# Moving statistics and a normalisation from VectorE to ScalarE in a four-layer convolution kernel, with a free choice of engine behind its long layer

## Chip, cores and metric

The kernel runs on one core of a Trainium2 chip. The metric is device time in microseconds (us), the median of several runs. The engines are named as the profile names them: PE (TensorE's matmuls; PEld is its weight loads), DVE (VectorE), ACT (ScalarE), POOL (GpSimd) and SP (SyncE, which here issues the DMAs).

## What is computed

The input is x of shape (8, 32, 256, 256): eight images of 32 channels. Four layers follow, each added to its own input, and each reads a group-normalised copy of it (mean and variance over two channels and the whole image):

```python
x = x + L0(gn(x), ...)   # 1x1 convolution, then a 5x5 filter per channel, pooled from the features
x = x + L1(gn(x), w)     # 8-bit quantised: out[f] = -sum over c, kh, kw of |patch - w|
x = x + L2(gn(x), w, b)  # 3x3 convolution
x = x + L3(gn(x), ...)   # layer norm over channels in 8x8 windows, then four networks k1..k4

def fastkan(x, ln_g, ln_b, ws, wb, bb):
    ln = layernorm(x, ln_g, ln_b)
    basis = exp(-((ln[..., None] - grid) / denom) ** 2)      # 8 grid points
    return flat(basis) @ ws.T + silu(x) @ wb.T + bb
```

In L3, k1 and k2 work on two rearranged views of the normalised window y, k3 on y itself. The sum of the three is z, k4 works on z, and the layer's output is k4(z) plus the window.

L1 quantises its input: scale, clip to -127..127 and round.

## The kernel before

An image is held as 128 partitions: four blocks of 64 rows by 32 channels. Work goes by chunks of 128 x 2048 (F = 2048 words a partition). Between stages an image lies in DRAM scratch (x1, x2, x3, and q for the quantised values). Four stages are built for each image:

- **Stage 0** (`stage0`, L729). First a statistics pass over the image in 8 chunks: `add_stats` (L637, four BN_STATS of 512 on DVE, recorded at L643) and `pool` (L746, five row reductions on DVE). Small matrices follow. Then 8 chunks of convolution: 25 taps on PE into the PSUM tile psB (L892), a border correction, an eviction on ACT (L925), `add_stats` on DVE, a store to x1. At the end the image is read back in 8 pieces, scaled on ACT (L967), clipped and rounded on DVE (L972, L973) and stored to q.
- **Stage 1**, layer 1 (`stage1`, L1027). There are 16 passes (4 row blocks h by 4 groups g of 8 output channels). A pass makes 72 distance tiles max(x - w, 0) of 128 x 4128 in bf16, on DVE (L996) or in two halves on ACT (L998). Each tile is summed over channels by 8 matmuls into psA (L1018). The residual is loaded into the buffer xr and added by matmul (L1007), psA is evicted into xr on ACT (L1065), two BN_STATS read xr, and it is stored to x2.
- **Stage 2**, layer 2 (`stage2`, L1090). 8 chunks are loaded with a margin row above and below (128 x 2560) and normalised on DVE (L1131); nine taps go into psB (L1148), ACT evicts (L1164), `add_stats` reads the result, and it is stored to x3.
- **Stage 3**, layer 3 (`stage3`, L1189). There are 8 units of one chunk. For each of five layer norms `variance` (L1225) centres by matmul (recorded at L612), evicts on ACT (L1234), squares on ACT (L1239) and sums by matmul into psV (L1247); `roots` (L1256) makes the inverse root by Ln and Exp on ACT; `scale` (L1268) spreads it by matmul (L1279) and multiplies on DVE (L1287). `kan` (L1349) then makes eight basis tiles: a square on ACT (L1384, or its substitute on DVE, L1390) and an exponential on ACT (L1397); eight main matmul groups (L612) and one for the silu part add up in psB, which ACT evicts (L1462). k3 adds two tiles `oa` and `od`, the outputs of k1 and k2, which are loaded back from DRAM once the fifth exponential is done (`after=exps[4:5]`, L1430).

**What orders the work.** Nothing is ordered by hand. `Plan.add` (L126) records a task with its engine, an assumed cost in us, the buffers it reads and writes, and a rank; `Plan.run` (L229) is a list scheduler that runs once while the kernel is built and fixes each engine's order. At each moment a free engine takes the ready task of lowest rank whose buffers fit. The ranks interleave stage 1 of image b with stages 2 and 3 of image b-1 and with stage 0 of later images. The distance tiles and their matmuls of stage 1 have no rank: `Plan.fill` (L357) gives them to DVE whenever no ranked task is ready there, to PE first of all once two finished tiles wait (`URGENT = 2`) and otherwise when nothing ranked is ready, and to ACT for image 0 or after ACT has had nothing ranked for 8 us. A task with a field `other` may go to a second engine, but only once all passes of stage 1, of all images, are done (L267).

**Buffers.** `ROOM` (L68) has three tiles "bas" for basis tiles, three "si", two "rs", one "xr", and an arena "sb" of 10 F words that is allocated in pieces; `NDV = 3` tiles "dv" hold distances. A basis tile that finds no "bas" tile goes into the arena if `BASE_SPARE` words remain besides (L171). psA, psB are one PSUM tile each, psV two. The first main matmul of a basis set waits until `exps[HOLD]` is done, with `HOLD = 4`, or until no basis tile is left (L1377). For the last image `parts` (L1219) centres and spreads through psA, in halves; for the others through psB.

The normaliser's statistics end in `Norm.finish` (L647): BN_AGGR on DVE (L656), then small matmuls and DVE operations give mean and inverse deviation.

Of the kernel before, what the change touches and what calls it, by code (L numbers as in the profile page):

```python
# [24 lines left out]
R = 8  # L25
# [42 lines left out]
ROOM = [("bas", 3 * BASE, BASE), ("si", 3 * F, F), ("rs", F // 2, F // 4), ("xr", F // 2, F // 2), ("sb", 10 * F, 0)]  # L68
AHEAD = 9.0
# [5 lines left out]
BASE_SPARE = 3 * F  # L75
HOLD = 4
# [14 lines left out]
class Buf:  # L91


    def __init__(self, kind, words=0):
        self.kind, self.words = kind, words
        self.writers, self.readers = [], []
        self.tile = None
        self.left, self.first, self.at, self.taken, self.base = 0, None, None, False, kind == "bas"
        self.spill = False
# [6 lines left out]
class Plan:  # L106
# [57 lines left out]
    def fits(self, need, spare):  # L164
# [3 lines left out]
        for b in need:  # L168
            if b.kind in ("dv", "bas") and b.spill:
                b.kind = "dv" if self.places["dv"] else "bas"  # L170
            if b.base:  # L171
                b.kind = "bas" if self.places["bas"] else "sb"
                spare = BASE_SPARE
            if b.kind in self.places and not self.places[b.kind]:
                return False
# [16 lines left out]
    def bases_full(self):  # L192
        return not self.places["bas"] and sum(n for _, n in self.free["sb"]) < F + BASE_SPARE

# [34 lines left out]
    def run(self):  # L229
# [23 lines left out]
        while left or any(not p.done for p in self.passes):  # L253
            moved = True
            while moved:
                moved = False
                for e in engines:
# [3 lines left out]
                    if best is None:  # L261
                        for t in ready[e]:
# [4 lines left out]
                            if t.eng != e and not all(p.done for p in self.passes[self.first_pass :]):  # L267
                                continue
# [4 lines left out]
                        if best is not None and e == "PE" and best.rank > self.image() + AHEAD:  # L273
                            piece = self.fill(e, False)
                            if piece is not None:
                                best = piece
                        if best is not None and best.n is not None:
                            ready[best.eng].remove(best)
                            if best.other:
                                ready[best.other[0]].remove(best)  # L280
                                if best.eng != e:
                                    self.sets[best.stretch][1] -= 1
# [71 lines left out]
    def image(self):  # L354
        return next((p.b for p in self.passes[self.first_pass :] if not p.done), len(self.passes))
# [92 lines left out]
def kernel(  # L448
# [142 lines left out]
    def sb(b, n=None):  # L591
        return b.tile[:, : n or b.words] if b.tile is not None else arena[:, b.at : b.at + (n or b.words)]
# [25 lines left out]
    class Norm:  # L618
# [17 lines left out]

        def add_stats(self, src, at, r, rank, n=4):  # L637
# [8 lines left out]

        def finish(self):  # L647
# [5 lines left out]
            def first():  # L653
                for i in range(n):
# [3 lines left out]
            plan.add("DVE", 1.1 if n == 1 else 1.5, first, r=self.bufs, w=[small], rank=self.rank)  # L658
# [70 lines left out]
    def stage0(b, rank, span, after):  # L729
# [9 lines left out]
        for k in range(NCH):  # L739
            xt = Buf("sb", F)  # L740
            plan.add(
                "SP", 2.0, lambda k=k, xt=xt: by_block(lambda p, q: nc.sync.dma_start(sb(xt)[p], xn[k, q])),
# [3 lines left out]
            def pool(k=k, xt=xt):  # L746
                v = sb(xt).rearrange("p (r w) -> p r w", w=W)
# [3 lines left out]
            norm.add_stats(xt, 4 * k, [], r(0.02 * k))  # L751
            plan.add("DVE", 2.9, pool, r=[xt], w=[rs_buf[k]], rank=r(0.02 * k))
# [103 lines left out]
        for k in range(NCH):  # L856
# [60 lines left out]
            for n, t in enumerate(tap_order):  # L917
# [7 lines left out]
                lambda xt=xt: nc.scalar.activation(  # L925
                    sb(xt, F), psB.rearrange("p s f -> p (s f)"), AF.Identity, bias=bi
# [3 lines left out]
            norm1.add_stats(xt, 4 * k, [], rk)  # L930
# [23 lines left out]
        for h in range(NH):  # L954
            for j in range(0, NJ, 2):
# [15 lines left out]
                def clip(t=t):  # L971
                    nc.vector.tensor_scalar(sb(t, F), sb(t, F), QMAX, -QMAX, ALU.min, ALU.max)  # L972
                    nc.vector.tensor_scalar(q16(t), sb(t, F), ROUND, ROUND, ALU.add, ALU.subtract)  # L973

                plan.add("DVE", 2.5, clip, w=[t], rank=rk)
# [51 lines left out]
    def stage1(b, x1buf, qbuf):  # L1027
# [3 lines left out]
        for h in range(NH):  # L1031
# [16 lines left out]
            for g in range(NG):  # L1048
# [3 lines left out]
                ps.xr = xr = Buf("xr", F // 2)  # L1052
# [4 lines left out]
                            sb(xr)[p],  # L1057
# [7 lines left out]
                    lambda g=g, xr=xr: nc.scalar.activation(  # L1065
                        sb(xr), psA.rearrange("p i f -> p (i f)"), AF.Identity, bias=wsum[:, g : g + 1]
# [6 lines left out]
                norm.add_stats(xr, 8 * g + 2 * h, [], rk, 2)  # L1073
# [5 lines left out]
                            sb(xr)[p],  # L1079
# [10 lines left out]
    def stage2(b, norm, x2buf, rank, span, after):  # L1090
        im = img[b]
        r = lambda f: rank + span * f
        wc, b2 = wt[:, K0 * K0 + 2, :], cc[:, 4:5]

        def fold():
# [3 lines left out]
            nc.vector.tensor_tensor(b2, norm.mean, col(B2), ALU.add)  # L1099

# [4 lines left out]
        for k in range(NCH):  # L1105
            xt, p = Buf("sb", 10 * W), Buf("psB")
# [3 lines left out]
            def load(k=k, xt=xt):  # L1110
                d = sb(xt)
# [18 lines left out]
            def normal(xt=xt):  # L1130
                nc.vector.tensor_scalar(sb(xt), sb(xt), norm.mean, norm.rs, ALU.subtract, ALU.mult)  # L1131

            plan.add("DVE", 1.7, normal, r=[norm.done], w=[xt], rank=rk)
# [23 lines left out]
            for n, t in enumerate(taps):  # L1157
# [6 lines left out]
                lambda xo=xo: nc.scalar.activation(sb(xo, F), psB.rearrange("p s f -> p (s f)"), AF.Identity, bias=b2),  # L1164
                r=[p, sm["c2"]], w=[xo], rank=rk,
            ))
            norm3.add_stats(xo, 4 * k, [], rk)
# [21 lines left out]
    def stage3(b, norm, x3buf, rank, span):  # L1189
# [26 lines left out]
        stat = {(k, t): (Buf("psV"), Buf("rs")) for t in range(-2, U + 2) for k in "ABC"}  # L1216
        turn = lambda t: r((t + 2) / (U + 4))
        st = [dict() for _ in range(U)]
        def parts():  # L1219

            if b < nb - 1:
# [3 lines left out]
        def variance(n, t, cen, bias, rk, src, sq=None):  # L1225
# [3 lines left out]
            for p, ps, i, us in parts():  # L1229
                at = slice(i * FS, (i + (2 if us < 1 else 4)) * FS)  # L1230
                plan.add("PE", 0.85 + 0.2 * us, lambda ps=ps, i=i: cen(ps(), i), r=src, w=[p], acc=[c], rank=rk, spare=SPARE)
                plan.add(
# [6 lines left out]
            plan.add("ACT", 1.9, lambda: nc.scalar.activation(sb(sq), sb(c), AF.Square), r=[c], w=[sq], rank=rk)  # L1239
            v = stat[t][0]  # L1240
# [52 lines left out]
        def front(t, after, rk):  # L1293
# [6 lines left out]
            st[t]["c4"] = variance(4, ("A", t - 1), cen, cb, rk, [xt, sm["cenf"], sm["c3"]], xt)  # L1300

        def middle(t):

            rk = turn(t - 1.0)
# [377 lines left out]
```

## Time and profile before

| | us |
|---|---|
| median of 3 runs | 15807.77 (15794.59 to 15817.06) |
| the profiled execution | 15810.7 |
| its span, first to last instruction | 15808.7 |
| PE, DVE, ACT busy | 12814.9, 13427.1, 12262.5 |
| BN_STATS on DVE (L643) | 637.3 |
| layer 2's normalisation on DVE (L1131) | 102.8 |
| the quantiser's clip and rounding on DVE (L972, L973) | 78.2, 78.5 |

In a row of groups the columns are: line, engine, operation, tiles out<-in, shapes, count | busy time, mean length of one in ns | idle time of the engine before them, and what ended it. Busy time can be less than count times mean, since neighbours overlap.

### The profile page before, as it was taken

The numbers are of one execution on the slowest core, as the hardware profiler recorded it, in microseconds if no ns is written. First come the engines' busy times: TensorE is split into PE (matmuls) and PEld (weight loads), VectorE is DVE, ScalarE is ACT, GpSimd is POOL, SyncE is SP. The second block draws the span as 40 slices with busy tenths as digits, with TensorE's granted clock in tenths as the row PEclk, the third lists the DMA queues.
The fourth block names the chain that finished last, engine by engine and source line by source line (L and its number), as shares of the span: only waits on it lengthen the run. The fifth ranks groups of instructions, "written<-read, shape, count | busy, mean of one in ns | idle before, by whom it ended". The sixth has DMA issues, their size and how long they took to land.

```text
span 15808.7 us, 560681 instructions
## 1 busy us (share of the span) xinstructions
PE 12814.9 (81%) x260296; PEld 4330.4 (27%) x260296; DVE 13427.1 (85%) x12536; ACT 12262.5 (78%) x6849; POOL 33.1 (0%) x25
## 2 busy tenths in 40 slices
PE   6889897887897888888887888778878887887666
PEld 4223232322222222223222222222222222222222
DVE  2898989789878889888899999999999989997465
ACT  0888848678648778676778997799879987997687
POOL 0000000000000000000000000000000000000000
PEclk9989898998998999999999999999999999998777
DMA  4342345446435444554545554454544454444554
GB/s 117 74 101 55 99 118 160 108 123 169 98 97 157 130 118 125 140 139 105 133 123 142 140 131 126 114 140 123 130 127 130 127 128 129 130 132 112 148 154 134
DMA packets 1192870, 1970.85 MB, mean 125 GB/s; under 512 B 362752, under 2 KB 878848, under 8 KB 1092224
## 3 DMA queue, kind: packets, MB, share of 16 engines
q1 hardware_dynamic: 1190528, 1934.98, 46.6%
q8 instruction: 2036, 33.36, 0.9%
q14 instruction: 306, 2.51, 0.1%
HBM read 1162.83 MB, written 771.75 MB: 122 GB/s over the span
## 4 chain that ended last, share of the span: by engine, by line
PE 22%; ACT 20%; DVE 6%; issue 6%; DMA 1%; SPq 0%; DVEq 0%; ACTq 0%
PE psB L612 9%; PE psA L1018 7%; ACT bas L1384 5%; ACT bas L1397 4%; DVE dv L996 3%; ACT arena L1384 2%; PE psB L1148 2%; ACT arena L1397 2%; ACT arena L1234 2%; PE psB L892 1%; ACT si L1462 1%; ACT arena L1239 1%; DVE arena L1287 1%; PE psV L1247 1%; DVE arena L1390 1%
## 5 line engine op out<-in xcount | busy, mean ns | idle before, releaser
L996 DVE TENSOR_SCALAR dv<-qh,w1q 128x4128 bf16<-128x4128 bf16 (+1 forms) x8815 | 10491.2, 1248 | 1358.8 <-PE psA L1018 1289.9
L1018 PE MATMUL psA<-dv,sel_b 128*32 128x512 bf16 x71048 | 5420.4, 403 | 1421.8 <-DVE dv L996 1155.5
L1018 PEld LDWEIGHTS <-sel_b 128*32 128x32 bf16 x82944 | 2047.6, 97 | 6763.7 <-issue 5758.6
L1384 ACT ACTIVATE bas<-arena,kb 128x2048 f32<-128x2048 f32 x1396 | 2782.5, 1993 | 411.8 <-DVE arena L1287 258.6
L1397 ACT ACTIVATE bas<-bas 128x2048 f32<-128x2048 f32 x1396 | 2671.6, 1914 | 40.1
L998 ACT ACTIVATE dv<-qh,w1n 128x2064 bf16<-128x2064 bf16 x832 | 1635.9, 2009 | 1157.6 <-PE psA L1018 1042.0
L612 PE MATMUL psB<-bas,tl 32*32 32x512 f32 x48544 | 1953.2, 653 | 438.8 <-ACT bas L1397 240.1
L892 PE MATMUL psB<-arena,wt 32*32 32x512 f32 (+1 forms) x51040 | 1848.8, 606 | 122.2 <-issue 69.4
L612 PE MATMUL psB<-arena,tl 32*32 32x512 f32 x22368 | 918.8, 619 | 104.0 <-ACT arena L1397 29.0
L612 PEld LDWEIGHTS psB<-bas,tl 32*32 32x32 f32 x48544 | 526.5, 107 | 1327.5 <-ACT bas L1397 514.2
L892 PEld LDWEIGHTS psB<-arena,wt 32*32 32x32 f32 x51040 | 657.5, 104 | 814.0 <-issue 611.4
L1384 ACT ACTIVATE arena<-arena,kb 128x2048 f32<-128x2048 f32 x407 | 810.0, 1990 | 0.0
L1397 ACT ACTIVATE arena<-arena 128x2048 f32<-128x2048 f32 x407 | 779.1, 1914 | 11.6
L643 DVE BATCH_NORM_STATS2 tiny<-arena 128x6 f32<-128x512 f32 x768 | 473.7, 680 | 345.4 <-ACT arena L925 246.4
L1018 PE MATMUL psA<-qh,sel_b 128*32 128x512 bf16 x9216 | 666.3, 394 | 92.1 <-DMA qh<-q 76.8
L1287 DVE TENSOR_TENSOR arena<-psB,arena 128x2048 f32<-128x2048 f32 x280 | 640.0, 2286 | 59.0 <-PE psB L1279 55.9
L1462 ACT ACTIVATE si<-psB,cols_sb 128x2048 f32<-128x2048 f32 x192 | 377.0, 1963 | 385.0 <-PE psB L612 331.5
L612 PE MATMUL psB<-si,tl 32*32 32x512 f32 x14080 | 618.8, 624 | 32.4 <-DVE arena L1287 13.8
L1148 PE MATMUL psB<-arena,tl 32*32 32x510 f32 (+3 forms) x16384 | 626.6, 610 | 19.9 <-issue 19.8
L1239 ACT ACTIVATE arena<-arena 128x2048 f32<-128x2048 f32 x320 | 612.4, 1914 | 9.8
L925 ACT ACTIVATE arena<-psB,cc 128x2048 f32<-128x2048 f32 x64 | 125.6, 1962 | 536.0 <-PE psB L913 536.0
L1234 ACT ACTIVATE arena<-psB 128x2048 f32<-128x2048 f32 x224 | 418.9, 1870 | 127.1 <-PE psB L612 126.5
(151 smaller groups left out, 7406.4 us busy)
## 6 DMA issues: line engine op xcount, KB each, us to landing
arena<-x SPq DMA_DIRECT2D x128, 1024.0 KB
arena<-y SPq DMA_DIRECT2D x128, 1024.0 KB
si<-sy SPq DMA_DIRECT2D x512, 256.0 KB
arena<-in_x_dram SPq DMA_DIRECT2D x240, 384.0 KB
arena<-in_x_dram SPq DMA_DIRECT2D x256, 256.0 KB
x<-arena SPq DMA_DIRECT2D x256, 256.0 KB
xr<-x SPq DMA_DIRECT2D x512, 128.0 KB
x<-xr SPq DMA_DIRECT2D x512, 128.0 KB
```

Of the source, the lines that this page charges most:

```text
L612: nc.tensor.matmul(view(o[j * C : (j + 1) * C, i - first, :]), w_, src(rows, i, j), start=start, stop=stop)
L892: nc.tensor.matmul(o[:, lo - 2 * j : hi - 2 * j, c0:c1], wt[rows, t, :], d[rows, lo + dy + 2 : hi + dy + 2, c0 + dx : c1 + dx], start=firs ...
L996: nc.vector.tensor_scalar(dst, src, w1q[:, at : at + 1], 0.0, ALU.subtract, ALU.max)
L998: nc.scalar.activation(dst, src, AF.Relu, bias=w1n[:, at : at + 1])
L1018: nc.tensor.matmul(psA[j * C : (j + 1) * C, i, :], sel_b[:, n, :], src[:, at : at + 2, t % 3 : t % 3 + W], **flags,)
L1148: nc.tensor.matmul(o[:, lo - 2 * j : hi - 2 * j, c0:c1], (wc if t == 4 else tl[:, W2T + t, :])[rows], d[rows, lo + dy + 1 : hi + dy + 1, c ...
L1234: lambda ps=ps, at=at: nc.scalar.activation(sb(c)[:, at], ps().rearrange("p s f -> p (s f)"), func, bias=shift),
L1239: plan.add("ACT", 1.9, lambda: nc.scalar.activation(sb(sq), sb(c), AF.Square), r=[c], w=[sq], rank=rk)
L1287: lambda ps=ps, at=at: nc.vector.tensor_tensor(sb(c)[:, at], ps().rearrange("p s f -> p (s f)"), sb(c)[:, at], ALU.mult),
L1384: lambda k=k, bas=bas: nc.scalar.activation(sb(bas), sb(rb), AF.Square, bias=kb[:, n, k : k + 1]),
L1397: lambda k=k, bas=bas, square=square: nc.scalar.activation(sb(bas), sb(bas), AF.Exp, scale=-1.0, bias=0.0 if square.eng == "ACT" else kbsq ...
L1462: nc.scalar.activation(sb(o), psB.rearrange("p s f -> p (s f)"), AF.Identity, bias=obias)
```

## The change

Statistics. `add_squares` takes the place of `add_stats`: the ACT evictions of stages 0, 1 and 2 also give the sum over their elements (`accum_out`), and a further ACT instruction squares the tile, shifted by the mean of the first chunk, and gives the sum of squares; its elementwise output is thrown into spare words behind the tile. In stage 0's first pass the sum comes from the row sums that the pooling makes anyway, less the columns that two bins share. `finish` builds mean and variance from these sums.

```diff
+        def add_squares(self, src, at, i, size, rank):
+            if not self.chunks & 1 << i:
+                self.chunks |= 1 << i
+                plan.add("DVE", 0.16,
+                    lambda: nc.vector.tensor_scalar(
+                        self.shift[:, i : i + 1], self.sums[:, at : at + 1], -1.0 / size, None, ALU.mult
+                    ), r=[src, self.summed], w=[self.shifted[i]], rank=rank)
+            plan.add("ACT", 0.25 + 0.85e-3 * size,
+                lambda: nc.scalar.activation(
+                    sb(src)[:, size : size + size // 2].bitcast(BF16), sb(src, size), AF.Square,
+                    bias=self.shift[:, i : i + 1], accum_out=self.squares[:, at : at + 1],
+                ), r=[src, self.shifted[i]], w=[self.bufs[at]], rank=rank)
...
-            norm.add_stats(xt, 4 * k, [], r(0.02 * k))
+                total, both = norm.sums[:, k : k + 1], norm.d[:, 0, 0:1]
+                nc.vector.tensor_reduce(total, rowsum[:, :, k * R : (k + 1) * R], AX.XY, ALU.add)
+                nc.vector.tensor_reduce(both, v[:, :, 51:205:51], AX.XY, ALU.add)
+                nc.vector.tensor_tensor(total, total, both, ALU.subtract)
+            norm.add_squares(xt, k, 0, F, r(0.02 * k))
...
-                    lambda g=g, xr=xr: nc.scalar.activation(
-                        sb(xr), psA.rearrange("p i f -> p (i f)"), AF.Identity, bias=wsum[:, g : g + 1]
+                    lambda g=g, h=h, xr=xr: nc.scalar.activation(
+                        sb(xr, F // 2), psA.rearrange("p i f -> p (i f)"), AF.Identity, bias=wsum[:, g : g + 1],
+                        accum_out=norm.sums[:, NH * g + h : NH * g + h + 1],
-                norm.add_stats(xr, 8 * g + 2 * h, [], rk, 2)
+                norm.add_squares(xr, NH * g + h, g, F // 2, rk)
```

The evictions L925 and L1164 change in the same way. Buffers grow for the thrown-away output: stage 0's chunk from F to 12 W words (3072), stage 2's from 10 W to 12 W, xr from F/2 to 3F/4.

Layer 2's input and the quantiser:

```diff
-                nc.vector.tensor_scalar(sb(xt), sb(xt), norm.mean, norm.rs, ALU.subtract, ALU.mult)
-            plan.add("DVE", 1.7, normal, r=[norm.done], w=[xt], rank=rk)
+                nc.scalar.activation(sb(xt, 10 * W), sb(xt, 10 * W), AF.Identity, bias=nmr, scale=norm.rs)
+            plan.add("ACT", 2.4, normal, r=[sm["c2"]], w=[xt], rank=rk)
...
-                    nc.vector.tensor_scalar(sb(t, F), sb(t, F), QMAX, -QMAX, ALU.min, ALU.max)
                     nc.vector.tensor_scalar(q16(t), sb(t, F), ROUND, ROUND, ALU.add, ALU.subtract)
-                plan.add("DVE", 2.5, clip, w=[t], rank=rk)
+                    nc.vector.tensor_scalar(q16(t), q16(t), QMAX, -QMAX, ALU.min, ALU.max)
+                plan.add("DVE", 1.95, clip, w=[t], rank=rk)
```

Behind layer 1 (`over()`: all passes done) centring may go to DVE, basis and silu tiles may take the distance buffers, and the last image asks for `oa` and `od` behind the first exponential. Two constants of the planner change for all images:

```diff
-BASE_SPARE = 3 * F
-HOLD = 4
+BASE_SPARE = 2 * F
+HOLD = 3
...
-                b.kind = "bas" if self.places["bas"] else "sb"
+                b.kind = "bas" if self.places["bas"] else "dv" if self.over() and self.places["dv"] else "sb"
+            if b.side:
+                b.kind = "si" if self.places["si"] or not self.over() else "dv" if self.places["dv"] else "sb"
...
+                evict.other = "DVE", 0.15 + 2.1 * us, lambda ps=ps, at=at: nc.vector.tensor_scalar(
+                    sb(c)[:, at], ps().rearrange("p s f -> p (s f)"), shift, None, ALU.add
+                )
+            square.other = "DVE", 2.3, lambda: nc.vector.tensor_tensor(sb(sq), sb(c), sb(c), ALU.mult)
...
-                        "SP", 2.0 if name == "oa" else 8.0, load2, r=[db], w=[a], rank=rk, after=exps[4:5], spare=F,
+                        "SP", 2.0 if name == "oa" else 8.0, load2, r=[db], w=[a], rank=rk, after=exps[(0 if last else 4) :][:1], spare=F,
```

The rest rewrites the loop over units without changing which task has which rank, and removes a comparison (`AHEAD = 9.0`) against ranks that never exceed it.

## Prediction

> **What bounds the kernel now.** I read the page first, then busy time by stretch, the groups by line, the waits, and the timeline of one unit at the end. On the page, no engine is full over the span:
>
> ```profile
> PE 12814.9 (81%) x260296; PEld 4330.4 (27%) x260296; DVE 13427.1 (85%) x12536; ACT 12262.5 (78%) x6849; POOL 33.1 (0%) x25
> ...
> PE   6889897887897888888887888778878887887666
> ...
> DVE  2898989789878889888899999999999989997465
> ACT  0888848678648778676778997799879987997687
> ```
>
> So stages must be told apart. L996 starts at 435 us and ends near 14490; L925 (stage 0's eviction) last runs at 7664, and layer 2 of image 3 begins at about 7720. That gives four stretches; the columns are length, then busy time of PE, PEld, DVE, ACT and POOL, then clock and DMA:
>
> ```profile
> 0.00:435.00 435.00, 241.20 (x6932) 167.70 (x6932) 131.89 (x375) 33.77 (x17) 1.17 (x10) 0.87 0.52 123
> 435.00:7720.00 7285.00, 6193.15 (x130770) 2081.81 (x130786) 6325.79 (x6412) 5399.34 (x2952) 20.33 (x8) 0.94 0.45 117
> 7720.00:14490.00 6770.00, 5515.41 (x106398) 1770.13 (x106366) 6248.10 (x5310) 5887.96 (x3305) 11.63 (x7) 0.94 0.49 129
> 14490.00:15809.00 1319.00, 865.13 (x16230) 310.76 (x16212) 721.34 (x441) 941.40 (x577) 0.00 (x0) 0.75 0.53 144
> ```
>
> Call them head, B (layer 1 beside stage 0), C (layer 1 beside stage 3 alone) and tail (the last image, behind layer 1). DVE is busy 87% of B, 92% of C and 55% of the tail. Its idle time in B and C has one cause, in the waits of B and then of C (total, times, longest):
>
> ```profile
> DVE dv L996 <- PE psA L1018: 824.5, 716, 26.2
> ```
> ```profile
> DVE dv L996 <- PE psA L1018: 465.4, 618, 5.3
> ```
>
> The distances wait until the matmuls have emptied a slot. B has two kinds of window, seen in image 0: without stage 0's convolution, and with it.
>
> ```profile
> 960.00:1120.00 160.00, 97.43 (x1214) 34.23 (x1229) 155.14 (x241) 147.59 (x79) 0.00 (x0) 0.70 0.63 171
> 1120.00:1600.00 480.00, 455.92 (x10362) 169.33 (x10343) 412.07 (x443) 411.23 (x219) 1.55 (x2) 0.99 0.25 55
> ```
>
> In the first DVE is full (97%) and PE at 61%; in the second PE is full (95%). DVE time is worth its length in the first, nearly nothing in the second. The work concerned:
>
> ```profile
> L996 DVE TENSOR_SCALAR dv<-qh,w1q 128x4128 bf16<-128x4128 bf16 (+1 forms) x8815 | 10491.2, 1248 | 1358.8 <-PE psA L1018 1289.9 <-issue 30.4 <-ACT dv L998 8.3
> L643 DVE BATCH_NORM_STATS2 tiny<-arena 128x6 f32<-128x512 f32 x768 | 473.7, 680 | 345.4 <-ACT arena L925 246.4 <-ACT arena L1164 73.1 <-DMA arena<-in_x_dram 21.5
> L643 DVE BATCH_NORM_STATS2 tiny<-xr 128x6 f32<-128x512 f32 x256 | 163.6, 681 | 24.5 <-ACT xr L1065 22.5 <-DMA si<-od 1.5
> L1065 ACT ACTIVATE xr<-psA,wsum 128x1024 f32<-128x1024 f32 x128 | 141.1, 1103 | 47.6 <-PE psA L1018 47.5
> L967 ACT ACTIVATE arena<-arena,cc 128x2048 f32<-128x2048 f32 x64 | 132.8, 2087 | 28.8 <-DMA arena<-x 28.8
> L1131 DVE TENSOR_SCALAR arena<-arena,tiny 128x2560 f32<-128x2560 f32 x64 | 102.8, 1608 | 25.1 <-DMA arena<-x 25.1
> L972 DVE TENSOR_SCALAR arena<-arena 128x2048 f32<-128x2048 f32 x64 | 78.2, 1222 | 17.1 <-ACT arena L967 16.6
> ```
>
> In the tail the DVE timeline shows a period; the bracket is idle time before:
>
> ```profile
> 15045.86 1.23 DVE L1287 TENSOR_TENSOR arena<-psA,arena 128x1024 f32<-128x1024 f32 x1 [27.55 <-PE psA L1279]
> ...
> 15173.74 1.23 DVE L1287 TENSOR_TENSOR arena<-psA,arena 128x1024 f32<-128x1024 f32 x1 [27.74 <-PE psA L1279]
> ```
>
> One unit takes 127.9 us, with a hole of 28 us on DVE in which the next unit's normalisers go through PE, ACT, PE, ACT in turn.
>
> **What the Trainium skill says.** "ScalarE: Activation LUTs", What ACT_TABLE_LOAD costs: an ACTIVATE takes 186 ns plus 0.833 ns an element, each pointer operand some 93 ns more. L967, with scale and bias as pointers, gives 186+1706+186 = 2078, measured 2087: it agrees. "VectorE: DVE Perf Modes", The perf-mode tier table: at 2048 elements tensor_scalar takes 1227 ns in fp32 and 693 in bf16. L972 shows 1222; the bf16 form at that size is not in the trace, but L996's forms (1291 for 4128, 753 for 2064) agree. Of the accumulator output the first page says only that it exists (What it computes), no price.
>
> **The change part by part**, made against the profiled execution: 15810.7 us, of which the span is 15808.7; the median of the runs is 15807.8, 3 us less.
>
> *DVE loses* L643, by stretch 52 (head), 402 (B), 160 (C) and 21 us (tail), and L1131, 1.61 us each: 39 in B, 51 in C, 13 in the tail. The second clip falls from 1.22 to 0.75 us: 56 in B save 26. *DVE gains* 0.53 us in each stage-0 chunk (two short reductions near 0.19 us by L819's 0.17, a subtraction of 0.16): 30 us in B; shifts and the new fold some 10 more in B, 3 in C. The aggregations (L656, 33 us) give way to about as many small operations: nothing. Net: B 402+39+26-40 = 427, C 160+51+4-3 = 212.
>
> *ACT gains*, per image: stage 0, 16 squares at 1.99 = 32 us; layer 1, 16 squares at 1.10 (L1065) = 18; layer 2, 8 squares at 1.99 = 16 and 8 normalisations of 2560 at 2.51 (L967 plus 512 x 0.833 ns) = 20; accumulator outputs, between 0 and 0.28 us each (a whole fixed part with one pointer), I take 0.2. A gain I exclude: it adds an output. With 24 outputs in stage 0 (8 evictions, 16 squares) and 48 in layers 1 and 2, that is 37 us and 63 us. In C: 4 x 63 = 252 against 134 us of distances on ACT (L998) that can be dropped.
>
> *Head:* some 12 us; the statistics shared DVE with the pooling, the loads remain.
>
> *B:* layer 0's input statistics (126 us, with the clips' 26 less the pooling's 30 = 122) lie in windows of the first kind and count in full. Layer 0's output statistics (138) lie beside the convolution, where PE is full: 0. The rest, 82+59+39 less 10 = 170, lies in mixed windows; bounds 0 and 1, I take 0.6: about 108. ACT's squares push out distances that ACT makes at 4.0 us apiece against DVE's 1.19: in image 0 three stage 0s and 18 us, 129/4.0 x 1.19 = 38 us; later ACT is idle a quarter of the time, so of the other 340 us only a quarter costs: 85/4.0 x 1.19 = 25. B: 122+108-63 = 167 saved.
>
> *C:* 212, taken at 0.8 since 465 us of waits for PE grow a little: 170. ACT's excess of 252-134 = 118 goes into 882 us of idle, most of it while layer 2 holds psB; I charge 35. The xr square is queued behind up to 2 us of exponentials, and who waits for it is only the next residual load into the single xr buffer, with a pass lasting about 105 us: nothing. C: 135 saved.
>
> *Tail:* two lines of a unit, from PE's and the DMA queue's timelines:
>
> ```profile
> 15106.17 12.67 SPq L1425 DMA_DIRECT2D si<-od  x16
> ```
> ```profile
> 15135.81 1.11 PE L1279 MATMUL psA<-rs,tl 32*32 32x512 f32 x8 [8.55 <-DVE arena L1287]
> ```
>
> `od` is asked for only behind the fifth exponential. Its matmuls stand behind this L1279, so the eviction at 15139.97, which starts the hole, comes about 9 us late. Behind the first exponential it can stand ahead. Letting DVE evict and square takes 2 to 3 us off the hole and evens ACT (107 us a unit) with DVE (79): 4 to 6 us. That is 15 to 18 a unit at best, 14 taken: 8 x 14 = 112 saved. The bounds are 0 and 8 x (127.9-103) = 200, 103 being all but 10% of the even share (107+79)/2 = 93. What is late next there is psB. The lent buffers and the smaller base reserve only make this possible; I give them nothing.
>
> *HOLD 3:* the first main matmul goes one square and exponential earlier, so psB is held up to 3.9 us longer per basis set. I cost it at nothing, since ACT (95% busy in C's full slices) is what paces the set; without that cover see rival 3. SP issues the same DMAs.
>
> Sum: 12+167+135+112 = 426; 15810.7-426 = 15385, in terms of the median 15382. I say **15382**. The rivals below are set against the median too.
>
> **The rivals.**
> *1. DVE is worth its length everywhere* (PE's queue follows DVE): 12+427+212 and a tail of 200 = 851, **14957**. For it: 92% in C. Against: PE at 95% beside the convolution.
> *2. PE takes over, and the tail's engine choice does little:* only 122-63 = 59 in B, 0 in C, 60 in the tail, 12 in the head: 131, **15677**. For it: the 824 us of waits for L1018. Against: in C, PE waits 773 us for L996.
> *3. ScalarE and psB bound stage 3, slower.* In C ACT has 882 us idle; at its best slices (378 of 400) 372 remain idle, so 510 can be used, with the 134 of L998 644. The new work takes 252, leaving 392: 98 an image, or 3.1 us for each of 32 basis sets. From there on HOLD's 3.9 us decides: in full it is 499, 107 too many, and stage 3 of image 6 ends 107 us after today's end of layer 1, with the tail as long as now: **15915**. For it: L1384 runs right up to 14490. Against: the hold runs beside ACT's own work.
>
> **How the numbers follow.** Forecast 0.56 (its own range 15160 to 15600), rival 1 0.17, rival 2 0.16, rival 3 0.11. A measurement of this kernel tells about 0.2%, 32 us, from no change. Rival 2 reaches into that with 0.04; so faster 0.56+0.17+0.12 = 0.85, same 0.04, slower 0.11. The range leaves out rival 3 and the far end of rival 1: 14930 to 15780.
>
> **What would show it.** Right: L643 gone; the last L996 near 14175; L996's waits for L1018 about as long in B although DVE has less to do; a unit of the tail near 114 us. Wrong: L996's waits growing by most of 640 us (rival 2); L1384 still running well past the last L996 (rival 3); or an accumulator output that shows a row of its own above 0.28 us.

## The result, and the profile after

The changed kernel takes 15622.67 us (median of 4 runs, 15617.2 to 15634.18) beside 15808.49 us for the kernel before: a ratio of 0.9884, with a 95% interval of 0.9867 to 0.9901. That is about 184 us saved, where 426 were forecast.

The page of the profile after gives the busy times:

```profile
PE 12717.2 (81%) x260296; PEld 4277.3 (27%) x260296; DVE 13113.9 (84%) x12066; ACT 12438.8 (80%) x7500; POOL 17.6 (0%) x25
```

DVE is 313 us less busy over the whole span. On ACT the 799 us of new work (the squares, the normalisation and the accumulator rows) come to 176 us more in all: distances there fall by 268 us, and behind layer 1 DVE takes over basis squares, centring squares and evictions. Line numbers have moved: the distances are L1041, their matmuls L1063, stage 3's evictions L1515, its spreading multiply L1342.

```profile
L1041 DVE TENSOR_SCALAR dv<-qh,w1q 128x4128 bf16<-128x4128 bf16 x8201 | 10125.5, 1292 | 1379.0 <-PE psA L1063 1331.7 <-issue 12.7 <-DMA qh<-q 6.8
L665 ACT ACTIVATE arena<-arena,tiny 128x2048 bf16<-128x2048 f32 x192 | 383.6, 1998 | 67.1 <-DMA arena<-in_x_dram 42.3 <-DVE tiny L658 22.0
L1178 ACT ACTIVATE arena<-arena,cc,tiny 128x2560 f32<-128x2560 f32 x64 | 159.8, 2512 | 0.0
L665 ACT ACTIVATE xr<-xr,tiny 128x1024 bf16<-128x1024 f32 x128 | 146.1, 1142 | 6.6 <-DVE tiny L658 5.0
L665 ACT ACTIVATION_READ_ACCUMULATOR arena<-arena,tiny 128x1 f32 x192 | 36.0, 188 | 0.0
L1018 DVE TENSOR_SCALAR arena<-arena 128x2048 bf16<-128x2048 bf16 x64 | 44.4, 694 | 2.2
```

The new rows cost what the forecast said: squares 1.998 and 1.142 us, the normalisation 2.512, an accumulator output 0.188 to 0.194, the bf16 clip 0.694. So the prices are not where it failed. The stretches are (length, then PE, PEld, DVE, ACT, POOL, clock and DMA; the last begins with the last distance):

```profile
0.00:425.00 425.00, 237.43 (x6932) 163.66 (x6932) 81.08 (x335) 76.29 (x65) 1.17 (x10) 0.88 0.52 122
425.00:10535.00 10110.00, 8647.24 (x179112) 2822.64 (x179113) 8928.50 (x8567) 8152.74 (x4934) 12.43 (x12) 0.95 0.47 122
10535.00:13951.00 3416.00, 2765.77 (x53292) 884.33 (x53287) 3062.82 (x2570) 3026.87 (x1800) 3.96 (x3) 0.94 0.48 129
13951.00:15632.00 1681.00, 1066.71 (x20964) 406.66 (x20964) 1041.49 (x596) 1182.87 (x704) 0.00 (x0) 0.74 0.54 144
```

Layer 1 ends with its last distance. Before (timeline of DVE):

```profile
14483.16 3.71 DVE L996 TENSOR_SCALAR dv<-qh,w1q 128x4128 bf16<-128x4128 bf16 x3 [0.32 <-PE psA L1018]
```

After:

```profile
13936.89 10.93 DVE L1041 TENSOR_SCALAR dv<-qh,w1q 128x4128 bf16<-128x4128 bf16 x9 [0.32 <-PE psA L1063]
```

So it ends at 13948 us instead of 14487, 539 us earlier and far more than forecast. But what follows it takes 1681 us instead of 1319. What happened in between is read from one store, the last output of image 6, that is, the end of stage 3 of the last image but one. Before (timeline of SP's queue):

```profile
14576.63 2.73 SPq L1479 DMA_DIRECT2D out_dram<-si  x4
```

After:

```profile
14522.69 2.75 SPq L1532 DMA_DIRECT2D out_dram<-si  x4
```

That moved by 54 us only. Before, stage 3 of image 6 ended 90 us behind layer 1 and hardly showed; now it ends 575 us behind it. The other 122 us of the 176 that the span lost come after this store (1232 us before, 1110 after), because layer 2 of image 7 has by then begun beside the leftover (its first eviction starts at 14194 us; before, at 14586, behind the store).

The leftover holds up image 7. The normaliser of image 7's layer 2 needs three matmuls in psB (L697, L709 and L734), and the tasks of image 6 go ahead of them, since they have the lower rank. Timeline after:

```profile
13990.45 0.17 DVE L683 TENSOR_REDUCE tiny<-tiny 128x4 f32<-128x16 f32 x1 [7.56 <-ACT xr L665]
...
14037.96 0.41 PE L697 MATMUL psB<-tiny,mats_sb 128*128 128x8 f32 x2
...
14115.77 0.60 PE L734 MATMUL psB<-tiny,mats_sb 128*128 128x8 f32 x2 [0.33 <-ACT arena L1285]
...
14124.27 0.16 DVE L1143 RECIPROCAL cc<-tiny 128x1 f32<-128x1 f32 x1
```

134 us pass from the first reduction to L1143 (before: 32, from 14516.2 to 14548.2). Between them psB is in use by image 6 nearly all the time.

psB is not an engine and has no row on the page, but it can be followed through the timeline, here in image 3 of the changed kernel:

```profile
5524.00 1.46 PE L613 MATMUL psB<-si,tl 32*32 32x512 f32 x32
...
5525.51 1.97 ACT L1515 ACTIVATE si<-psB,cols_sb 128x2048 f32<-128x2048 f32 x1 [2.44 <-PE psB L613]
...
5527.53 1.15 PE L613 MATMUL psB<-arena,tl 32*32 32x512 f32 x32 [0.65 <-ACT si L1515]
5528.85 1.88 ACT L1285 ACTIVATE arena<-psB 128x2048 f32<-128x2048 f32 x1 [1.38 <-PE psB L613]
...
5530.79 1.15 PE L1195 MATMUL psB<-arena,wt 32*32 32x512 f32 x32 [0.35 <-ACT arena L1285]
...
5546.88 1.97 ACT L1211 ACTIVATE arena<-psB,cc 128x2048 f32<-128x2048 f32 x1 [7.70 <-PE psB L1195]
```

The evictions of a basis set's sum, of a centring and of a layer-2 chunk follow each other here. The basis set leaves psB at 5527.48 and a centring enters at 5527.53; that leaves at 5530.73 and layer 2 enters at 5530.79. Nothing lies between. I add up every use from its first matmul to the end of the read that empties it (1064 uses): psB is held 13251 us of the kernel before, about as long as DVE is busy there, and 13416 us of the kernel after, longer than any engine works. In the layer-1 stretches that have stage 0 beside stage 3 (images 2 and 3 before, 2 to 5 after) it is held 91 to 93% of the time; beside images 6 and 7, where no stage 0 is left, it is 81 to 83% in both kernels. Held is not the same as worked in: nearly half of the held time, some 6400 us, belongs to the 256 basis sets, which keep psB for 25 us each on average, until ACT has made their last exponentials and emptied it.

How far stage 3 runs behind layer 1 shows what that does. I take the end of layer 1 of an image (its last eviction into xr) and the end of stage 3 of the image before it (its last store). For image 3 before the change (timelines of ACT and of SP's queue):

```profile
7607.27 1.11 ACT L1065 ACTIVATE xr<-psA,wsum 128x1024 f32<-128x1024 f32 x1
...
8451.44 2.75 SPq L1479 DMA_DIRECT2D out_dram<-si  x4
```

For image 5 after it:

```profile
10534.20 1.09 ACT L1110 ACTIVATE xr<-psA,wsum 128x1024 f32<-128x1024 f32 x1
...
11534.10 2.73 SPq L1532 DMA_DIRECT2D out_dram<-si  x4
```

Before, the distance is 844 us at image 3 and shrinks from there: 685, 526, 355 and 89 at image 7. After, it is 743 at image 3, still grows to 902 and 1000, and shrinks only then, to 835 and 573. In both kernels it shrinks once stage 0 is through, whose last eviction starts at about 7667 us before and at 10062 after. The leftover at the end is what stage 3 had no time to catch up.

### The profile page after: what moved, and what is told of

Same layout as the page of the kernel before. It is cut to its first block, busy times and chain, and to the rows that moved or that the text cites. A ratio compares the mean times of both kernels' runs of the same rounds, so it can differ in the third digit from the quotient of the medians.

```text
span 15632.3 us, 560441 instructions
## 1 busy us (share of the span) xinstructions
PE 12717.2 (81%) x260296; PEld 4277.3 (27%) x260296; DVE 13113.9 (84%) x12066; ACT 12438.8 (80%) x7500; POOL 17.6 (0%) x25
## 5 line engine op out<-in xcount | busy, mean ns | idle before, releaser
L1041 DVE TENSOR_SCALAR dv<-qh,w1q 128x4128 bf16<-128x4128 bf16 (+1 forms) x8831 | 10545.8, 1254 | 1395.2 <-PE psA L1063 1347.3
L1063 PE MATMUL psA<-dv,sel_b 128*32 128x512 bf16 x70800 | 5339.6, 400 | 1229.3 <-DVE dv L1041 1033.5
L1063 PEld LDWEIGHTS <-sel_b 128*32 128x32 bf16 x82944 | 2035.5, 96 | 6498.0 <-issue 5467.4
L1437 ACT ACTIVATE bas<-arena,kb 128x2048 f32<-128x2048 f32 x1367 | 2724.8, 1993 | 338.2 <-DVE arena L1342 270.7
L1450 ACT ACTIVATE bas<-bas 128x2048 f32<-128x2048 f32 x1367 | 2615.5, 1913 | 38.5
L1043 ACT ACTIVATE dv<-qh,w1n 128x2064 bf16<-128x2064 bf16 x668 | 1319.4, 2010 | 1069.6 <-PE psA L1063 1036.7
L613 PE MATMUL psB<-arena,tl 32*32 32x512 f32 x18432 | 736.1, 614 | 139.1 <-ACT si L1515 44.8
L1342 DVE TENSOR_TENSOR arena<-psB,arena 128x2048 f32<-128x2048 f32 x280 | 640.6, 2288 | 217.6 <-PE psB L1334 212.2
L1063 PE MATMUL psA<-qh,sel_b 128*32 128x512 bf16 x9216 | 668.9, 387 | 88.3 <-DMA qh<-q 73.4
L1437 ACT ACTIVATE arena<-arena,kb 128x2048 f32<-128x2048 f32 x353 | 702.5, 1990 | 0.2
L1450 ACT ACTIVATE arena<-arena 128x2048 f32<-128x2048 f32 x353 | 675.7, 1914 | 10.2
L1195 PE MATMUL psB<-arena,tl 32*32 32x512 f32 (+3 forms) x16384 | 635.1, 613 | 31.0 <-issue 30.7
L1515 ACT ACTIVATE si<-psB,cols_sb 128x2048 f32<-128x2048 f32 x191 | 374.5, 1961 | 299.5 <-PE psB L613 273.6
L1293 ACT ACTIVATE arena<-arena 128x2048 f32<-128x2048 f32 x289 | 552.9, 1913 | 8.4
L1334 PE MATMUL psB<-rs,tl 32*32 32x512 f32 x8960 | 349.6, 648 | 215.1 <-DVE arena L1342 110.0
```

The source lines that it names most:

```text
L613: nc.tensor.matmul(view(o[j * C : (j + 1) * C, i - first, :]), w_, src(rows, i, j), start=start, stop=stop)
L1041: nc.vector.tensor_scalar(dst, src, w1q[:, at : at + 1], 0.0, ALU.subtract, ALU.max)
L1043: nc.scalar.activation(dst, src, AF.Relu, bias=w1n[:, at : at + 1])
L1063: nc.tensor.matmul(psA[j * C : (j + 1) * C, i, :], sel_b[:, n, :], src[:, at : at + 2, t % 3 : t % 3 + W], **flags,)
L1195: nc.tensor.matmul(o[:, lo - 2 * j : hi - 2 * j, c0:c1], (wc if t == 4 else tl[:, W2T + t, :])[rows], d[rows, lo + dy + 1 : hi + dy + 1, c ...
L1293: square = plan.add("ACT", 1.9, lambda: nc.scalar.activation(sb(sq), sb(c), AF.Square), r=[c], w=[sq], rank=rk)
```

## Experiments

Three theories stood against each other. **S:** stage 3 sets the end, held up by psB, so relieving DVE only ends layer 1 earlier. **D:** DVE's time was worth what was forecast, and another part of the change costs the rest. **A:** ScalarE's added work holds stage 3 up. The planner's own clock, which some expectations use, is the end of its list of tasks by its assumed costs (`self.span`). All runs in one table; times in us, the ratio is to the kernel before with its interval, "image 6" is the store shown above, psB is the time held:

| run | ratio | last distance | image 6 | span | psB |
|---|---|---|---|---|---|
| before | 1 | 14487 | 14577 | 15809 | 13251 |
| after | 0.9884 (0.9867–0.9901) | 13948 | 14523 | 15632 | 13416 |
| moves_alone | 0.9945 (0.9930–0.9959) | 13839 | 14605 | 15719 | 13523 |
| tail_alone | 1.0004 (0.9995–1.0012) | 14500 | 14600 | 15812 | 13157 |
| after_old_constants | 0.9926 (0.9909–0.9942) | 13817 | 14574 | 15665 | 13399 |
| moves_new_constants | 0.9901 (0.9886–0.9916) | 13943 | 14513 | 15652 | 13449 |
| acc_squares_short | 0.9876 (0.9861–0.9891) | 13906 | 14505 | 15615 | 13320 |
| fewer_distances | 0.9793 (0.9779–0.9808) | 13333 | 14395 | 15486 | 13366 |
| fewer_taps | 0.9674 (0.9657–0.9690) | 14035 | 14058 | 15298 | 12149 |
| order_shuffled | 0.9909 (0.9894–0.9924) | 13846 | 14575 | 15671 | 13378 |
| fewer_sums | 0.9908 (0.9891–0.9924) | 14189 | 14459 | 15646 | 13144 |
| two_moves_back | 0.9876 (0.9862–0.9891) | 13992 | 14489 | 15602 | 13347 |
| psb_first | 0.9865 (0.9851–0.9880) | 14333 | 14381 | 15585 | 12916 |
| psb_first_two_moves_back | 0.9696 (0.9681–0.9710) | 14078 | 14129 | 15319 | 12737 |

**The change in parts.**

moves_alone: statistics, normalisation, clip and buffer sizes as changed, the rest as before (the same lending of "dv" tiles is also taken out of `bases_full`).

```diff
-BASE_SPARE = 2 * F
-HOLD = 3
+BASE_SPARE = 3 * F
+HOLD = 4
...
-                evict.other = "DVE", ...
-            square.other = "DVE", ...
...
-... "dv" if self.over() and self.places["dv"] else "sb"
+... "sb"
...
-after=exps[(0 if last else 4) :][:1]
+after=exps[4:5]
```

> The moves of statistics, normalisation and clip alone: HOLD 4, BASE_SPARE 3 F and the end behind layer 1 as before (no second engine for centring, no lent buffers, od behind the fifth exponential). Theory S (stage 3 sets the end: it runs behind layer 1, held up by psB, so that DVE's relief brings only layer 1's end forward): 15700 to 15800 us, with the last distance near 13900 and stage 3 of image 6 ending 500 us or more behind it. Theory D (DVE's time was worth what the forecast said, and another part of the change costs the rest): 15809 - 12 - 167 - 135 = 15495. Theory A (ScalarE's added work of some 500 us is what delays stage 3): also near 15750, so this run does not part S from A.

Measured: 15711.41 us. Layer 1 ends 648 us earlier, stage 3 of image 6 28 us later. All that is gained lies behind that store. Theory D would have 15495 and falls.

tail_alone: the reverse, statistics, normalisation, clip, buffer sizes and constants as before, the parts behind layer 1 as changed.

> The parts behind layer 1 alone (second engine for centring and its square, lent distance buffers, oa and od behind the first exponential of the last image); statistics, normalisation, clip, buffer sizes, HOLD and BASE_SPARE as before. The forecast gave these parts 112 us: 15697. From the unit of the changed kernel (some 126 us against 127.9, eight units) the gain would be 15 to 50: 15760 to 15795.

Measured: 15805.82 us, no difference. Both expectations had a gain that did not come.

after_old_constants: the first four lines of the diff above, nothing else.

> The changed kernel with HOLD 4 and BASE_SPARE 3 F. The forecast costed both at nothing: 15623. Theory S, if what counts is only that psB is held up to 3.9 us longer per basis set with HOLD 3: faster, 15450 to 15600. Theory S, if basis tiles that wait for room are what lets psB stand idle: slower, by the 161 us that the planner's own clock gives, near 15785.

Measured: 15671.51 us, a ratio 0.0042 above that of the changed kernel. The two constants together seem to matter, in the direction of basis tiles that wait for room, at under half of the planner's price. Which of the two does it was not tried.

moves_new_constants: moves_alone with HOLD 3 and BASE_SPARE 2 F.

> The moves with HOLD 3 and BASE_SPARE 2 F, but none of the parts behind layer 1. The forecast's value of those parts: 15623 + 112 = 15735. Theory S: the planner's own clock gives 80 us more than the changed kernel: near 15700; against the moves alone the two constants then show what they are worth when DVE has been relieved (planner's clock: 147).

Measured: 15643.58 us, better than expected. Against moves_alone the constants are worth 0.0044, some 70 us, and image 6 shows it: 14513 for 14605. Adding the parts behind layer 1 gives another 0.0017, less than the two intervals can tell.

**Which resource.**

acc_squares_short (the planner's assumed cost of such a square falls with its size):

```diff
-sb(src)[:, size : size + size // 2].bitcast(BF16), sb(src, size), AF.Square, ...
+sb(src)[:, size : size + size // 16].bitcast(BF16), sb(src, size // 8), AF.Square, ...
-q, 1.0 / count, d,
+q, 8.0 / count, d,
```

> The changed kernel with every statistics square over an eighth of its elements (its sum multiplied by 8, so the variances are estimates and the output is another): ScalarE does 192 x 1.5 + 128 x 0.75 = 380 us less, VectorE, TensorE and the use of psB are untouched. Theory A (ScalarE's added work holds stage 3 up): 250 to 350 us faster, 15270 to 15370. Theory S (psB holds stage 3 up): less than 60 us faster, 15565 to 15625. Theory D: nothing, 15623.

Measured: 15618.11 us. ACT is busy 279 us less (12160 for 12439), and the time is the same; theory A falls.

fewer_distances (the counts of a pass are adjusted to it):

```diff
-self.terms = [(o, t) for t in range(9) for o in range(OG)]
+self.terms = [(o, t) for t in range(9) for o in range(OG) if o or t > 2]
```

> The changed kernel with 3 of the 72 distance tiles of a pass left out (their terms are missing from layer 1): VectorE does 3 x 128 x 1.19 = 457 us less, TensorE some 3 x 128 x 8 matmuls less. Theory D (VectorE's time is worth its length): 350 to 450 us faster, 15170 to 15270. Theory S: layer 1 ends 450 to 550 us earlier, stage 3 of image 6 ends where it did, and the whole is at most 110 us faster: 15510 to 15620.

Measured: 15485.29 us. Layer 1 ends 615 us earlier, image 6 only 128 us, the whole 144 us by the ratios. That is more than S allowed (110) and far less than D asked for (350): of what layer 1 gains, about a quarter reaches the whole. Why a quarter is not shown; TensorE, too, is busy 201 us less here (12516 for 12717).

fewer_taps:

```diff
-for n, t in enumerate(tap_order):
+for n, t in enumerate(tap_order[:16]):
```

> The changed kernel with 16 of the 25 taps of stage 0's convolution (9 are missing from the output): psB is held some 9 x 1.0 us less in each of 64 chunks, 56 of them beside stage 3: 500 us and more; VectorE and ScalarE are untouched. Theory S: the whole gets shorter by half of that or more, 15280 to 15400. Theories A and D: TensorE is no bound while layer 1 runs beside stage 3, so at most 60 us, from image 0: 15560 or later.

Measured: 15301.00 us, 332 us faster by the ratios. psB is held 1267 us less, stage 3 of image 6 ends 465 us earlier and only 23 us behind layer 1, although layer 1 ends 87 us later. This run also relieves TensorE (busy 12252 us for 12717), and lets 35 chunks of stage 0 instead of 24 run beside image 0, so that stage 0 is through by 6330 us; hence the next.

fewer_sums (the count of a pass's matmuls is adjusted to it):

```diff
-self.sums = list(range(9))
+self.sums = []
-self.left = 9 + OG * 9
+self.left = OG * 9
```

> The changed kernel without the nine gathers of the unshifted input in each pass (their term is missing from layer 1): TensorE does 9 x 128 x 8 matmuls less, psB, VectorE and ScalarE do what they did. It parts TensorE from psB, which the run with fewer taps relieved together. If TensorE's time is the bound: 300 us or more faster, below 15320. Theory S (psB, not TensorE): less than 80 us either way, 15540 to 15700.

Measured: 15652.20 us, no gain in the whole, with TensorE busy 336 us less (12381 for 12717). It isn't clean, though: the planner put more of stage 0 beside image 0 (32 chunks for 24), so that layer 1 of that image ended at 1962 us for 1662, and the rest was 286 us shorter, with 8 x 47 us of psB moved out of it. By itself this run doesn't part TensorE from psB; for that see the last run below.

order_shuffled:

```diff
-us = (0.05 + 1.24 * (hi - lo) / RH) if e == "DVE" else ...
+us = (0.05 + 1.20 * (hi - lo) / RH) if e == "DVE" else ...
```

> The changed kernel with one assumed cost of the planner 3 per cent smaller (a distance on VectorE 0.05 + 1.20 us for 0.05 + 1.24): the same work in a slightly different order. It shows how much the order alone scatters the time. All theories: within 60 us of 15623; if it is further off, differences of that size between other runs prove nothing.

Measured: 15665.59 us, 0.0025 above the changed kernel for the same work. Its last distance comes 102 us earlier and its store of image 6 52 us later. So differences of some 40 us between two orders, among them the parts behind layer 1 and two_moves_back below, prove nothing by themselves, and the 66 to 70 us of the two constants, found twice, are not far above that.

**From the cause to a better kernel.**

two_moves_back: layer 1's statistics (BN_STATS of xr) and layer 2's normalisation on DVE again.

```diff
-norm.add_squares(xr, NH * g + h, g, F // 2, rk)
+norm.add_stats(xr, 8 * g + 2 * h, [], rk, 2)
-nc.scalar.activation(sb(xt, 10 * W), sb(xt, 10 * W), AF.Identity, bias=nmr, scale=norm.rs)
+nc.vector.tensor_scalar(sb(xt, 10 * W), sb(xt, 10 * W), norm.mean, norm.rs, ALU.subtract, ALU.mult)
```

> The changed kernel with layer 1's statistics (BN_STATS of xr) and layer 2's normalisation back on VectorE, the rest as changed. ScalarE does about 340 us less, VectorE about 265 us more. Theory S: neither engine sets the end, so within 50 us of 15623 (the planner's own clock gives 4 us). Theory D: 150 us or more slower. Theory A: 150 us or more faster.

Measured: 15604.30 us. DVE is busy 176 us more than in the changed kernel (13290 for 13114) and the time stands within the scatter, where theory D asked for 150 us more: D falls here too.

psb_first: evictions of psB by layer 2, centring and spreading get rank -0.5, so that on their engine they go ahead of all but layer 1's own evictions (rank -1.0), and BASE_SPARE becomes 0. (The second pair of lines stands twice in the kernel, for centring and for spreading.)

```diff
-r=[p, sm["c2"]], w=[xo], rank=rk,
+r=[p, sm["c2"]], w=[xo], rank=-0.5,
...
-r=[p], w=[c], rank=rk,
+r=[p], w=[c], rank=-0.5,
...
-BASE_SPARE = 2 * F
+BASE_SPARE = 0
```

> The changed kernel with the evictions of psB by layer 2, centring and spreading ahead of all else on their engine, and with no reserve in the arena for basis tiles (BASE_SPARE 0). Theory S: psB is free sooner, but both engines' queues behind these evictions stay as long; the planner's own clock gives 3 us: 15560 to 15650, with stage 3 of image 6 ending some 90 us earlier.

Measured: 15589.23 us, 33 us less than the changed kernel and within the scatter. No work is taken away; psB is held 500 us less, and stage 3 of image 6 ends 142 us earlier, 48 us behind layer 1. But layer 1 now ends 385 us later. The timeline shows a cause of that:

```profile
13687.44 1.13 ACT L665 ACTIVATE xr<-xr,tiny 128x1024 bf16<-128x1024 f32 x1
...
13688.69 1.72 SPq L1101 DMA_DIRECT2D xr<-x  x4
...
13693.28 1.95 PE L1052 MATMUL psA<-xr,mats_sb 128*128 128x512 f32 x4
...
13695.33 1.12 ACT L1110 ACTIVATE xr<-psA,wsum 128x1024 f32<-128x1024 f32 x1
...
13697.25 1.29 DVE L1041 TENSOR_SCALAR dv<-qh,w1q 128x4128 bf16<-128x4128 bf16 x1 [35.84 <-PE psA L1063]
```

The square at 13687.44 belongs to the pass that was evicted at 13554.23: it stood 133 us behind stage 3's work on ACT. The one xr buffer is held so long; only then is the next residual loaded (L1101), added (L1052), the next pass evicted (L1110), and a distance starts after 35.8 us of waiting. In 45 of 128 passes here the square ends over 40 us after its eviction; in the changed kernel in 24, at most 144 us; with BN_STATS on DVE in none (at most 13 us before).

psb_first_two_moves_back: both edits.

> Both together: evictions of psB first, no reserve for basis tiles, layer 1's statistics and layer 2's normalisation back on VectorE. Theory S: what helps is whatever lets stage 3 of image 6 end nearer to layer 1's end; here the planner's own clock has it 343 us earlier than in the changed kernel, and layer 1 175 us later, so the whole near 15623 - 256 = 15370, at worst 15500. Theory D: slower than the changed kernel, since VectorE gets 265 us of work back.

Measured: 15323.47 us, a ratio of 0.9696 to the kernel before and about 300 us faster than the changed kernel, where neither edit alone gives more than 33 us. psB is held 12737 us, stage 3 of image 6 ends 51 us behind layer 1, and layer 1 ends 255 us earlier than in psb_first. It beats both kernels. From its page:

```profile
PE 12658.3 (83%) x260296; PEld 4283.7 (28%) x260296; DVE 13090.7 (85%) x12203; ACT 12390.8 (81%) x7213; POOL 29.9 (0%) x25
```

In the changed kernel these were 12717, 13114 and 12439. For nearly the same work of each engine the time is 300 us shorter, so the amount of work on none of them was what set it. Stage 0 is through at about the same time as there (its last eviction starts at 9859 for 10062), so this run is free of what blurs fewer_taps. Two things are not parted in it: the earlier evictions of psB from BASE_SPARE 0, and layer 1's statistics from layer 2's normalisation. And psB's held time alone does not tell the gain: psb_first has 500 of the 679 us less, but 33 of the 300 us.

## Why the prediction was wrong

The sign was right and the mechanism on DVE too; the size was less than half. Step by step:

- **Head**, 12 us: the first distance starts at 428.9 instead of 435.4, about half of it.
- **B and C**, 167 + 135. As a statement on layer 1 this was too cautious: 314 us were forecast with the head, 539 measured, and 648 with the moves alone, close to DVE's whole relief (12 + 427 + 212 = 651). That the two agree within 3 us is partly luck, since a reordering alone moved this end by 102. Still, the weights 0, 0.6 and 0.8 and the charges for ACT (63 and 35) made the forecast for layer 1 too small. (0.6 of 170 is 102, not the 108 in the working; the sum would be 420 instead of 426.)
- **The step that failed** is the sum. It takes what layer 1 gains as gained by the whole, with the stretch behind it unchanged but for its own edits. That holds only if stage 3 of image 6 ends with layer 1. The trace before showed that it already ended 90 us later (14577 against 14487), after being 844 us behind in the middle. A faster layer 1 could only leave it further behind. With the moves alone layer 1 gains 648 us, stage 3 of image 6 nothing (28 us later), and the whole some 88; with the whole change it is 539, 54 and 184.
- **"ACT's excess of 118 goes into 882 us of idle"**: the forecast asked whether ACT has room. It has: 279 us less on ACT bring nothing. What has next to no room is psB, as long as stage 0's convolution shares it (held 91 to 93% of the time). The forecast named psB as next in the tail, but did not add up how long it is held. The Trainium skill, "Perfetto Trace Analysis", Matmuls, advises that independent matmul groups rotate through different PSUM banks, so that one is emptied while the next is filled; the timeline above, where a use of psB starts 0.05 us after the last read of the one before, is the case in which they don't. No run here tried a second tile.
- **Tail**, 112: nothing when made alone, and a ratio of 0.0017 on top of the rest, less than can be told. The mis-sized term is the hole, of which the forecast took 14 us a unit off. DVE's wait ahead of the spreading multiply does shrink, since DVE now evicts in it (timeline of the changed kernel):

```profile
14975.36 1.23 DVE L1342 TENSOR_TENSOR arena<-psA,arena 128x1024 f32<-128x1024 f32 x1 [9.83 <-PE psA L1334]
...
15101.87 1.23 DVE L1342 TENSOR_TENSOR arena<-psA,arena 128x1024 f32<-128x1024 f32 x1 [9.65 <-PE psA L1334]
```

  But 27.7 us to 9.7 is only the bracket. From one basis set to the next psB still stands empty for some 31 us once a unit (31.3, before 31.0): the chain of normalisers is as long on two engines as on one. ACT and DVE did come nearer to each other (97 and 90 us a unit for 106 and 81), but a unit takes 126.5 us for 127.9.
- **HOLD 3 and BASE_SPARE 2 F** "at nothing": together worth 0.0044, 70 us, beside the moves. The forecast costed HOLD against psB alone. That the constants help because basis tiles wait less for room fits the sign, but was not shown, and their shares were not tried apart.
- **The xr square**, "nothing": not so. The forecast had it wait for up to 2 us of exponentials; it ends 21 us after its eviction on average and up to 144. In the changed kernel that costs little, since stage 3 ends later still (two_moves_back takes the delay away and gains 18 us). Once stage 3 is quicker, as in psb_first, layer 1's end matters, and with the two moves taken back it comes 255 us sooner.
- **Rivals.** Rival 1 was right on layer 1 with the moves alone (651 for 648) and wrong on the end. Rival 2's time (15677) is the nearest, but for the wrong reason. Its sign, the distances' waits for layer 1's matmuls growing by most of 640 us, did not come (1289.9 us before, 1347.3 after), and the last run gained 300 us with TensorE's work nearly the same. Rival 3 named the place, stage 3 of image 6 running behind layer 1 through psB, and the sign that would show it. Its price was wrong: it reckoned from ACT's idle time and charged HOLD as a loss, and had the leftover make the whole slower. The leftover takes back part of a gain; it does not exceed it.
- **A reading.** The forms of L996, said to agree with the quoted 693 ns, share its slope but not its length (753 ns at 2064 elements). The clip, for which it was used, came out at 694.

What stays open: why the planner now spreads stage 0 over images 1 to 5 (before, its convolution was through by 7667 us), and how much of stage 3's delay that alone makes. DVE's relief is one candidate. The buffers are another, which no run tried: every run with the moves also has the chunk of stage 0's first pass at 3072 words instead of 2048, and it is loaded only when these and FUTURE = 5 F words more are free in the arena of 10 F. fewer_taps and fewer_sums moved the end of stage 0 along with what they were meant to move. So the runs show that an earlier end of layer 1 alone does not bring the end of the whole forward by as much, since stage 3 ends behind it; that psB is what holds stage 3 up is supported by fewer_taps and by the last run, but not isolated.

## What to carry to other kernels

Before pricing a faster engine, find the second chain and when it ends: here one store in the timeline showed that stage 3 already ended 90 us too late. A buffer that several stages take in turn is a resource like an engine; add up its time from first write to last read, stage by stage, and compare it with the engines' busy time. When a step is moved to another engine, ask what buffer it keeps meanwhile: the square itself was short, its place in ACT's queue was not.

## What the runs showed of the hardware

An accumulator output shows as a row of its own, ACTIVATION_READ_ACCUMULATOR, 0.188 to 0.194 us each, the same for tiles of 1024 and 2048 elements: 576 of them make 109 us on ACT. The same work in another order, made by a change of 3% in one assumed cost, took 0.25% longer, about as much as several of the edits here.
